# VectorE's one-column reads of kept numbers take a zero from a PSUM bank as their other operand, stand at every step of the left direction too, and are left out of the first 64 steps

## The chip, the cores and the metric

The kernel runs on one core of one Trainium2 chip. The metric is the device time of one execution in microseconds; lower is better. The median of the runs is what is compared.

## The reference, cut to what matters

Four residual layers work on `x` of shape (4, 48, 256, 256), each behind a group norm of 16 groups. Layer 0 is channel attention with a depthwise convolution, layer 1 a gated convolution. Layers 2 and 3 are the ones that the change touches. Both are four scans, one after the other, in which each row or column is the input plus a convolution of five taps along the row or column made just before:

```python
def step(w, b):
    def f(carry, inp):
        nxt = inp + _conv1d(carry, w, b)      # 48 channels to 48, 5 taps
        return (nxt, nxt)
    return f
_, d_rest = scan(step(down_w, down_b), xs[0], xs[1:])         # down, row by row
_, u_rest = scan(step(down_w, down_b), u0, seq)               # up
_, r_rest = scan(step(right_w, right_b), r0, ws[1:])          # right, column by column
_, l_rest = scan(step(left_w, left_b), l0, R[Ww - 2::-1])     # left
x = x + _L2_conv_ref(_gn(x), ...)                             # and the same for layer 3
```

No step of a scan can start before the step ahead of it is done. Each of the four directions has 255 steps, in each of the two layers.

## The kernel before, in words

`layers01` computes the first two layers; its last third overlaps with the beginning of `scans`. `scans` holds layers 2 and 3 (called layer 0 and 1 inside it) as two **chains**: `chain(0)` carries images 0 and 1, `chain(1)` images 2 and 3. Each chain is a generator; `next` on it emits one step. Chain 0 is emitted `lead = 992` steps ahead of chain 1, then both alternate, and chain 1 does its last steps alone, beside `to_rows(0, ...)`, which reorders chain 0's finished output with copies on GpSimd and ScalarE (`oo<-oi`). A planner reorders the emitted instructions on each engine by priority and dependence; the order on each engine is then fixed.

One **step** (`step`) works on the two images of a pair one after the other. For each image, called its first and second half here, TensorE runs three matmuls of 96x128 (in float32 each shows as two records) into a bank of PSUM, and VectorE adds the input to the result and writes it to a `carry` tile (`carry<-ps,dn`, `carry<-ps,up` at L1068; `carry<-ps,pre`, `carry<-ps,lines` at L1072). The matmuls of the next step read that `carry`. There are `NC = 4` carry tiles for a chain, used in turn, so a carry may be overwritten only when everybody has read it. What else reads it depends on the direction:

- down and up: ScalarE writes carry plus bias over the input row (`dn<-carry`, `up<-carry`);
- right: GpSimd first copies the column out of the block into a small tile `pre` (L1259), VectorE adds it, ScalarE writes the line (`lines<-carry`, L1286). Chain 0 has three `pre` tiles, chain 1 four;
- left: GpSimd adds the carry into the block `stage` in place (L1334, 96x256 for both images). In the second layer of chain 1 (`direct`), it adds into `done` instead, one 96x128 add for each image (L1338), and `out<-done` is stored from there. In the first layer, VectorE also takes statistics of the finished block of 16 columns (`st<-stage`, eight instructions for a block).

Around these steps stand **looks**: VectorE instructions on one column whose result, `seen`, nobody uses. A look reads a number that ScalarE or GpSimd has written, so VectorE waits for that engine once there, and the planner then need not give the same wait to VectorE instructions behind it. `look(place, fetched)` keeps the last places in a list and reads the oldest when more than three are kept: a copy (L1039) in down and up, and in right one add (L1041) of the old line and of the `pre` tile that the next step needs. In left, not in `direct`, every second step has a copy of its own (L1348).

```python
kept.append(place)
if len(kept) > 3:
    if fetched is None:
        nc.vector.tensor_copy(seen, kept.pop(0))
    else:
        nc.vector.tensor_add(seen, kept.pop(0), fetched)
```

Of the kernel before, what the change touches and what calls it, by code (L numbers as in the profile page):

```python
# [9 lines left out]
F32 = mybir.dt.float32  # L10
# [3 lines left out]
PSUM = bass.MemoryType.PSUM  # L14
DRAM = bass.MemoryType.DRAM

B, C, H, W = 4, 48, 256, 256
G = 16
NP = 2
P = 96  # L20
# [944 lines left out]
def scans(ctx, tc, xs, out, wts, biases, dram, k, coefs, lead, spare):  # L965
# [13 lines left out]
    nc = tc.nc  # L979
# [3 lines left out]
    pool = lambda name, bufs, **how: ctx.enter_context(  # L983
        tc.tile_pool(name=name, bufs=bufs, reuse_waits="tile", **how)
    )
# [6 lines left out]
    slots_d = pool("c_slot_d", 5)  # L992
    p_small = pool("c_ps", 1, space=PSUM)
    psum = pool("c_psum", 2, space=PSUM)
    sums = [spare, psum]
    buffers = [Ring([slots_a] * 3 + [slots_c, slots_b]), Ring([slots_d] * 5)]
    NT = H // RT
    NH = RT // 2
    CB = 2 * KC
# [16 lines left out]
    def take(pair, name):  # L1016
        return buffers[pair].tile([P, SLOT], F32, tag="slot", name=name)

    def chain(pair):
# [7 lines left out]
        seen = wp.tile([P, 1], F32, tag=f"seen{pair}", name="seen")  # L1027
        kept = []

        def look(place, fetched=None):  # L1030

            kept.append(place)
            if len(kept) > 3:
                if fetched is None:
                    nc.vector.tensor_copy(seen, kept.pop(0))  # L1039
                else:  # L1040
                    nc.vector.tensor_add(seen, kept.pop(0), fetched)  # L1041

        def slot(name):
            return take(pair, f"{name}{pair}")

        def inner():
            return carry[at[0]][:, :, 1 : HP - 1]
# [5 lines left out]
        def blocks(v):  # L1053
            return v.rearrange("p b (k w) -> p b k w", w=KC)
# [30 lines left out]
        def row(ts, r):  # L1085
            return rows_view(ts[r % 2])[:, :, :, r // 2, :]

        def load_rows(layer, n, r, t, k0, k1):

            v = rows_view(t)  # L1090
            for b in range(2):
                for q in range(2):
                    nc.sync.dma_start(
                        v[q * C : (q + 1) * C, b, k0:k1].rearrange("c k h w -> c k (h w)"),
                        xs[layer][pair][
                            r * C : (r + 1) * C, b, 2 * k0 + q : 2 * k1 - 1 + q : 2, n * NH : (n + 1) * NH, :
                        ].rearrange("c k h w -> c k (h w)"),
                    )

        def layer_of(layer, first):  # L1100
# [18 lines left out]
            def norm(t, b):  # L1119
                v = by_batch(t)[:, b]  # L1120
                g = biased[b]
                nc.scalar.activation(v, v, AF.Identity, bias=g[:, 1:2], scale=g[:, 0:1])
# [11 lines left out]
            for n in range(NT):  # L1134
                ahead_ = None
                for r in range(RT):
                    if r == 0:
                        kept.clear()
                        while len(halves) < min(2 * n + 5, 2 * NT):
                            t = slot("dn")  # L1140
                            load_rows(layer, len(halves) // 2, len(halves) % 2, t, 0, NK)
                            halves.append(t)
                        if n + 1 < NT:
                            ahead_ = halves[2 * n + 2 : 2 * n + 4]
                    if ahead_ and r in (11, 14, 22, 25):
                        norm(ahead_[r // 22], r % 11 // 3)
                    inp = row(now, r)

                    def keep(new, b):
                        nc.scalar.activation(inp[:, b], blocks(new[:, b]), AF.Identity, bias=bias[:, 0:1])  # L1150

                    if n == 0 and r == 0:
                        keep(inner(), slice(0, 2))
                    else:
                        step(layer, 0, inp, keep)
                    look(inp[:, 1, 0, 0:1])
                    yield
                if ahead_:
                    for r in range(2):
                        nc.sync.dma_start(D[n][r], now[r])  # L1160
                    now = ahead_
# [90 lines left out]
            fetched = {}  # L1252
# [59 lines left out]
            direct = layer == 1 and pair == NP - 1  # L1312
            done = None
            writes = []
            for n in reversed(range(NK)):
                ahead_ = None
                if direct and n % 2 == 1:
                    done = [take(0, "done") for _ in range(2)]
                for w in reversed(range(CB)):
                    if w == CB - 1 and n > 0:  # L1320
                        ahead_ = slot("lines"), slot("stage")
                        nc.sync.dma_start(ahead_[0], Rt[n - 1])
                        nc.sync.dma_start(by_batch(ahead_[1]), block_of(x, n - 1))
                    if layer == 0 and n == 0 and w == CB // 2:
                        following = [slot("dn"), slot("dn")]
                        for r in range(2):
                            load_rows(1, 0, r, following[r], 1, NK)
                    line = lines_view(lines)[:, w]
                    to = cols_view(stage)[:, :, w % 2, :, w // 2]

                    def keep(new, b):
                        if not direct:
                            if b.stop == 2:
                                nc.gpsimd.tensor_add(to, to, new)  # L1334
                            return
                        for i in range(b.start, b.stop):
                            place = done[i].rearrange("p (h w) -> p h w", w=2 * CB)[:, :, n % 2 * CB + w]
                            nc.gpsimd.tensor_add(place, to[:, i], new[:, i])  # L1338

                    if n == NK - 1 and w == CB - 1:  # L1340
                        keep(inner(), slice(0, 2))
                    else:
                        step(layer, 2, line, keep)
                    if not direct and w % 2:

                        kept.append(to[:, 1, H // 2 - 1 :])
                        if len(kept) > 1:
                            nc.vector.tensor_copy(seen, kept.pop(0))  # L1348
                    if late:
                        late.pop(0)()  # L1350
                    if writes and w % 8 == 4:
                        writes.pop(0)()
                    yield
                if layer == 0:
                    nc.sync.dma_start(block_of(y, n), by_batch(stage))
                elif not direct:
                    v = stage.rearrange("p (b q t n) -> p b q t n", b=2, q=2, t=NY)
                    for b in range(2):
                        for q in range(2):
                            nc.sync.dma_start(result[:, b, :, 2 * n + q], v[:, b, q])  # L1360
                elif n % 2 == 0:

                    def write(b, r, done=done, w0=n * CB):
                        at_rows = out[(2 * pair + b) * C : (2 * pair + b + 1) * C].rearrange(
                            "c (h r w) -> c h r w", r=2, w=W
                        )
                        nc.sync.dma_start(
                            at_rows[:, :, r, w0 : w0 + 2 * CB],
                            done[b][r * C : (r + 1) * C].rearrange("c (h w) -> c h w", w=2 * CB),
                        )  # L1370

                    writes += [lambda b=b, r=r, f=write: f(b, r) for b in range(2) for r in range(2)]
                if layer == 0:

                    def stat(b, c, n=n, v=by_batch(stage)):
                        nc.vector.bn_stats(stats[b][:, n * 4 + c, :], v[:, b, c * 512 : (c + 1) * 512])

                    late += [lambda b=b, c=c, f=stat: f(b, c) for b in range(2) for c in range(4)]
                    if n == 0:
                        for r in range(2):  # L1380
                            for q in range(2):
                                nc.sync.dma_start(
                                    rows_view(following[r])[q * C : (q + 1) * C, :, 0].rearrange("c b h w -> c b (h w)"),
                                    cols_view(stage)[r * C : (r + 1) * C, :, q, :NH, :].rearrange("c b h w -> c b (h w)"),
                                )
                if ahead_:
                    lines, stage = ahead_
# [211 lines left out]
```

## Time and profile before

| What | Value |
|---|---|
| Median of 3 runs | 9099.63 us (9092.13 to 9106.2) |
| Profiled execution, its own time | 9105.24 us |
| Its span, first to last instruction | 9103.5 us |
| Mean granted TensorE clock | 0.984 |
| TensorE matmuls busy | 8713.5 us, 96% of the span |
| VectorE busy | 3971.3 us, 44% |
| ScalarE busy | 3440.2 us, 38% |
| GpSimd busy | 1948.2 us, 21% |
| Looks: L1039, L1041, L1348 | 1852, 1008 and 381 instructions |

The page gives busy time by engine, then the span in 40 slices, then groups of instructions by line with their count, busy time, mean duration and what ended the idle time ahead of them. PE is TensorE, PEld its weight loads, DVE VectorE, ACT ScalarE, POOL GpSimd, SP the queue that issues transfers. Chain 0 begins at about 3200 us beside the end of the second layer and is the only work from about 3600 to 5000 us but for a few steps of chain 1; both chains run from about 5000 to 7750 us; chain 1 is alone from there to the end.

### The profile page before, as it was taken

How to read it: one execution, taken by the hardware profiler on the slowest of the kernel's cores; microseconds unless marked ns; L12 is line 12 of the kernel's file. 1: busy time of each engine (PE TensorE's matmuls, PEld its weight loads, DVE VectorE, ACT ScalarE, POOL GpSimd, SP SyncE). 2: the span in 40 equal slices, each digit the busy share in tenths (PEclk: the TensorE clock that was granted, in tenths of full speed). 3: DMA queues.
4: the chain of work that ended last, by engine and by line, in shares of the span. 5: the costliest groups of instructions: out<-in, count | busy, mean ns of one | idle time of the engine just before them, and what ended most of it. 6: DMA issues, size and time to landing. Idle time of an engine off the chain costs nothing. (4 is left out here: it accounts for less than half of the span.)

```text
span 9103.5 us, 158554 instructions
## 1 busy us (share of the span) xinstructions
PE 8713.5 (96%) x62920; PEld 7234.4 (79%) x62920; DVE 3971.3 (44%) x14031; ACT 3440.2 (38%) x7023; POOL 1948.2 (21%) x3100
## 2 busy tenths in 40 slices
PE   6999999999999978999999999999999999999998
PEld 4777777433333336999888999999999999999998
DVE  3232010234555555444345544444444555444543
ACT  0011000123343455765400776666554002765610
POOL 0000000001111120002444000001445664001566
PEclk9999999999999988999999999999999999999999
DMA  7664323467878877765466755465556787867789
GB/s 150 132 133 89 71 62 73 94 137 168 180 171 179 180 159 163 161 143 143 119 168 165 168 140 135 116 152 134 161 158 163 215 224 175 204 168 191 210 171 184
DMA packets 1180201, 1390.37 MB, mean 153 GB/s; under 512 B 263184, under 2 KB 1107216, under 8 KB 1118784
## 3 DMA queue, kind: packets, MB, share of 16 engines
q1 hardware_dynamic: 1179360, 1379.90, 64.9%
q8 instruction: 493, 8.08, 0.4%
q14 instruction: 252, 2.06, 0.1%
q0 software_dynamic: 96, 0.33, 0.0%
HBM read 811.21 MB, written 509.61 MB: 145 GB/s over the span
## 5 line engine op out<-in xcount | busy, mean ns | idle before, releaser
L1064 PE MATMUL ps<-carry,w 96*96 96x128 f32 x48960 | 5490.2, 274 | 115.0 <-DVE carry L1072 71.7
L1064 PEld LDWEIGHTS ps<-carry,w 96*96 96x96 f32 x48960 | 5407.4, 163 | 207.4 <-DVE carry L1072 134.7
L1259 POOL COPY pre<-col 96x256 f32<-96x256 f32 x1020 | 656.7, 644 | 2755.5 <-DMA col<-last 1971.7
L1150 ACT ACTIVATE dn<-carry,b 96x128 f32<-96x128 f32 (+1 forms) x2044 | 769.1, 398 | 838.3 <-DVE carry L1068 828.9
L1286 ACT ACTIVATE lines<-carry,b 96x128 f32<-96x128 f32 (+1 forms) x2044 | 780.2, 399 | 690.8 <-DVE carry L1072 650.1
L1068 DVE TENSOR_TENSOR carry<-ps,dn 96x128 f32<-96x128 f32 x2280 | 652.5, 287 | 755.8 <-PE ps L1064 730.5
L1194 ACT ACTIVATE up<-carry,b 96x128 f32<-96x128 f32 x1792 | 719.1, 402 | 459.8 <-DVE carry L1068 456.3
L1068 DVE TENSOR_TENSOR carry<-ps,up 96x128 f32<-96x128 f32 x1792 | 516.0, 288 | 598.9 <-PE ps L1064 594.1
L1334 POOL TENSOR_TENSOR stage<-stage,carry 96x256 f32<-96x256 f32 x768 | 656.2, 856 | 527.4 <-DVE carry L1072 497.5
L1072 DVE TENSOR_TENSOR carry<-ps,lines 96x128 f32<-96x128 f32 x2040 | 547.6, 283 | 424.9 <-PE ps L1064 401.1
L581 PE MATMUL py<-x1n,wy 128*96 128x512 f32 x1536 | 703.6, 607 | 30.4 <-ACT x1n L541 27.9
L1072 DVE TENSOR_TENSOR carry<-ps,pre 96x128 f32<-96x128 f32 x2040 | 550.9, 284 | 271.1 <-PE ps L1064 239.7
L295 PE MATMUL acc<-xs,xt 128*96 128x288 f32 x2048 | 666.7, 407 | 0.0
L294 PE MATMUL acc<-xt 128*96 128x288 f32 x2048 | 666.5, 409 | 0.0
L581 PEld LDWEIGHTS py<-x1n,wy 128*96 128x96 f32 x1536 | 245.2, 166 | 455.2 <-issue 437.0
L279 DVE COPY xt<-pt 128x384 f32<-128x384 f32 x256 | 136.6, 554 | 850.8 <-PE pt L276 650.3
L261 ACT ACTIVATE xn<-raw,coef 96x2048 f32<-96x2048 f32 x64 | 133.6, 2094 | 987.6 <-PE pt L276 819.6
L296 PE MATMUL acc<-xt,xs 128*96 128x192 f32 x2048 | 501.7, 327 | 0.0
L296 PEld LDWEIGHTS acc<-xt,xs 128*96 128x96 f32 x2048 | 332.1, 165 | 154.3 <-issue 1.4
L295 PEld LDWEIGHTS acc<-xs,xt 128*96 128x96 f32 x2048 | 332.0, 164 | 151.2 <-issue 2.2
L604 DVE TENSOR_TENSOR y<-py,t 96x512 f32<-96x512 f32 x256 | 171.4, 678 | 600.8 <-PE py L590 600.8
L1041 DVE TENSOR_TENSOR seen<-lines,pre 96x1 f32<-96x1 f32 x1008 | 166.8, 165 | 479.6 <-POOL pre L1259 437.2
(183 smaller groups left out, 5520.3 us busy)
## 6 DMA issues: line engine op xcount, KB each, us to landing
stage<-x SPq DMA_DIRECT2D x64, 1536.0 KB
dn<-x SPq DMA_DIRECT2D x240, 384.0 KB
R<-lines SPq DMA_DIRECT2D x60, 1536.0 KB
lines<-R SPq DMA_DIRECT2D x60, 1536.0 KB
D<-dn SPq DMA_DIRECT2D x56, 1536.0 KB
up<-D SPq DMA_DIRECT2D x56, 1536.0 KB
U<-up SPq DMA_DIRECT2D x224, 384.0 KB
col<-U SPq DMA_DIRECT2D x56, 1536.0 KB
```

The source lines that it names most:

```text
L294: nc.tensor.matmul(acc[0], lhsT=xt[:, h + 2, :], rhs=xt[:, here, :], start=first, stop=last)
L295: nc.tensor.matmul(acc[1], lhsT=xt[:, h + 2, :], rhs=xs[:, here, :], start=first, stop=last)
L296: nc.tensor.matmul(acc[2], lhsT=xs[:, h + 2, :], rhs=xt[:, past, :], start=first, stop=last)
L581: nc.tensor.matmul(ps, lhsT=held["w"][0][:, dx], rhs=x1n[:, 2 * c : 2 * c + 2, dx : dx + W], start=dx == 0, stop=False)
L1064: nc.tensor.matmul(ps, lhsT=w_sb[layer][:, way, j, :], rhs=old[:, i, j : j + W // 2], start=j == 0, stop=j == 2)
L1068: nc.vector.tensor_add(new[:, i].rearrange("p (k w) -> p k w", w=KC), ps.rearrange("p (k w) -> p k w", w=KC), inp[:, i])
L1072: nc.vector.tensor_add(new[:, i], ps, inp[:, i])
L1150: nc.scalar.activation(inp[:, b], blocks(new[:, b]), AF.Identity, bias=bias[:, 0:1])
L1194: nc.scalar.activation(place[:, b], blocks(new[:, b]), AF.Identity, bias=bias[:, 1:2])
L1259: nc.gpsimd.tensor_copy(t, cols_view(block)[:, :, w % 2, :, w // 2])
L1286: nc.scalar.activation(line[:, b], new[:, b], AF.Identity, bias=bias[:, 2:3])
L1334: nc.gpsimd.tensor_add(to, to, new)
```

## The change

A pool with one bank of PSUM is added, and one column of it is set to zero. A look becomes `tensor_add(seen, zero, number)`, with one number of SBUF and the zero from PSUM. Where a look read two numbers (right), it becomes two looks, one for the old line and one for the `pre` tile; the latter now starts with the first step of the direction. In left, the copy at every second step becomes a look at every step, with the list of more than three kept places, on the first row of the column, and there are looks in `direct` too, which had none. The looks of the first 64 steps of chain 0 (down, first layer) are left out.

```diff
     p_small = pool("c_ps", 1, space=PSUM)
     psum = pool("c_psum", 2, space=PSUM)
+    p_zero = pool("c_zero", 1, space=PSUM)
     sums = [spare, psum]
+    zero = p_zero.tile([P, 1], F32, tag="zero", name="zero")
+    nc.vector.memset(zero, 0.0)
...
             kept.append(place)
-            if len(kept) > 3:
-                if fetched is None:
-                    nc.vector.tensor_copy(seen, kept.pop(0))
-                else:
-                    nc.vector.tensor_add(seen, kept.pop(0), fetched)
+            old = [kept.pop(0)] if len(kept) > 3 else []
+            for number in old + ([] if fetched is None else [fetched]):
+                nc.vector.tensor_add(seen, zero, number)
...
                         step(layer, 0, inp, keep)
-                    look(inp[:, 1, 0, 0:1])
+                    if pair or layer or n > 1:
+
+                        look(inp[:, 1, 0, 0:1])
                     yield
...
                         step(layer, 2, line, keep)
-                    if not direct and w % 2:
-
-                        kept.append(to[:, 1, H // 2 - 1 :])
-                        if len(kept) > 1:
-                            nc.vector.tensor_copy(seen, kept.pop(0))
+                    if direct:
+                        look(done[1].rearrange("p (h w) -> p h w", w=2 * CB)[:, 0, n % 2 * CB + w : n % 2 * CB + w + 1])
+                    else:
+                        look(to[:, 1, 0:1])
                     if late:
                         late.pop(0)()
```

## The prediction

> **What bounds the kernel now.** I read the busy times first, then the groups, then the timeline of each stage, since the scans have stages with different limits.
>
> ```profile
> PE   6999999999999978999999999999999999999998
> ...
> L1064 PE MATMUL ps<-carry,w 96*96 96x128 f32 x48960 | 5490.2, 274 | 115.0 <-DVE carry L1072 71.7
> L1334 POOL TENSOR_TENSOR stage<-stage,carry 96x256 f32<-96x256 f32 x768 | 656.2, 856 | 527.4 <-DVE carry L1072 497.5
> L1041 DVE TENSOR_TENSOR seen<-lines,pre 96x1 f32<-96x1 f32 x1008 | 166.8, 165 | 479.6 <-POOL pre L1259 437.2
> ```
>
> TensorE is the bound nearly everywhere: the scan matmuls fill 5490 us and wait 115 us. A VectorE instruction of 0.15 us costs nothing by its own length. What counts is whether a look holds VectorE so long that TensorE runs out of carries. So I read the left direction with both chains, chain 0 in the second layer and chain 1 in the first, in order of time:
>
> ```profile
> 7201.06 0.15 DVE L1348 COPY seen<-stage 96x1 f32<-96x1 f32 x1 [0.97 <-POOL stage L1334]
> 7201.13 0.47 DVE L1072 TENSOR_TENSOR carry<-ps,lines 96x128 f32<-96x128 f32 x2
> 7201.69 0.85 POOL L1334 TENSOR_TENSOR stage<-stage,carry 96x256 f32<-96x256 f32 x1 [0.66 <-DVE carry L1072]
> 7202.57 0.15 DVE L1348 COPY seen<-stage 96x1 f32<-96x1 f32 x1 [0.97 <-POOL stage L1334]
> 7202.64 0.73 DVE L1072 TENSOR_TENSOR carry<-ps,lines 96x128 f32<-96x128 f32 x3
> ...
> 7205.42 0.85 POOL L1334 TENSOR_TENSOR stage<-stage,carry 96x256 f32<-96x256 f32 x1 [0.46 <-DVE carry L1072]
> 7206.31 0.15 DVE L1348 COPY seen<-stage 96x1 f32<-96x1 f32 x1 [0.97 <-POOL stage L1334]
> ```
>
> A look waits 0.97 us for a GpSimd add that began only when the two carries just ahead of the look were done. Look, two carries, add, look: 7201.06 to 7202.57, **1.51 us**. Behind the waiting look stand the other chain's two carries. The looks come every second step: 7201.06 to 7206.31 is 5.25 us for two joint steps (a step of either chain), 2.625 us each, and 24 matmul records of 0.109 us are just that. The steps without looks let VectorE catch up, so TensorE never waits.
>
> The end of the kernel, `direct` left of chain 1 alone, has no looks:
>
> ```profile
> 8850.94 0.29 DVE L1072 TENSOR_TENSOR carry<-ps,lines 96x128 f32<-96x128 f32 x1 [0.39 <-PE ps L1064]
> 8851.31 0.52 POOL L1338 TENSOR_TENSOR done<-stage,carry 96x128 f32<-96x128 f32 x1 [0.15 <-DVE carry L1072]
> 8851.61 0.29 DVE L1072 TENSOR_TENSOR carry<-ps,lines 96x128 f32<-96x128 f32 x1 [0.38 <-PE ps L1064]
> 8851.98 0.52 POOL L1338 TENSOR_TENSOR done<-stage,carry 96x128 f32<-96x128 f32 x1
> ```
>
> Carries follow at 0.67 us, 1.35 us a step, set by TensorE; GpSimd trails and nobody waits for it. Last, the right direction of chain 1 alone, where the other chain's output is reordered:
>
> ```profile
> 8487.45 1.12 POOL L1448 COPY oo<-oi 96x1024 f32<-96x1024 f32 x1
> 8487.54 1.03 DVE L1041 TENSOR_TENSOR seen<-lines,pre 96x1 f32<-96x1 f32 x1 [0.15 <-POOL pre L1259]
> ```
>
> The look, 0.156 us in the median, takes 1.03 us because a GpSimd copy began 0.09 us before it.
>
> [...] a carry, one input from PSUM, keeps its 0.29 us beside GpSimd's `pre` copies. [...] `gn_m<-pg`, one column from PSUM, has a median of 0.146 us against 0.140 for a `seen` copy. I take 0 for the operand [...].
>
> **The change, part by part.** The order in which the changed program's instructions stand, with the instruction that each look waits for, decides. GpSimd's order is unchanged; TensorE, ScalarE and SP differ only at the start of chain 0, where three more of its steps (and some loads of `dn`) stand ahead of the last piece of the layer before. No store or load moves past the looks elsewhere.
>
> 1. *Left with both chains.* Though the source keeps three places back, in the changed order nearly every look waits for the GpSimd add of the step just made, and now both chains have one at every step: look, two carries of chain 0, look, two carries of chain 1. The loop above then closes: 2 x 1.51 = 3.02 us against TensorE's 2.625, +0.395 us. 207 joint steps have chain 0 and chain 1 both in left. Some 35 of them lie beside the statistics (0.68 us each, eight a block) with fewer tight looks; following their order by the same durations I get 12.3 us for four, 3.07 each, so I price all 207 alike: **+82 us**. TensorE now waits for carries; the add on GpSimd is what is late next.
>
> 2. *`direct` left.* 219 of the new looks wait for the second `done` add of the step just made. From a carry's start: 0.37 to GpSimd's start (8850.94 to 8851.31), two adds back to back 1.00 (the trace has such a pair at 8789.08), 0.03 to the look, 0.07 to the carry: 1.47 against 1.35. +0.12 x 219 = +26. Against it, the transfers of this stage run at 98% to 100% of their engines and GpSimd waits 30 us for `stage`; a slower stage gets part of that back, I take 4. **+22 us** (0 to +45: fully hidden by transfers, or each late `stage` block felt at once, where today carries run ahead).
>
> 3. *Left of chain 0 alone.* Today a look at every second step; the cycle of two steps is 3.25 us (looks at 4600.84 and 4604.09), above TensorE's 2.63. With a look at every step, the extra one delays only a first half: its carry starts at 1.58 after the earlier look, not 1.34, while the second half waits for its own matmuls until 1.99, as before. So the next look is again at 3.25. **0**, 0 to +15.
>
> 4. *Right.* Chain 0 alone has a cycle of 3.10 us for two steps, set by a look on the `pre` just copied; this stays. The second look stands between the two carries, 0.08 us, in a step whose other half waits 0.28 us for TensorE. **0**, 0 to +13. With both chains, one tight look is left in a joint step and the loop is near 2.1 us, under 2.6: **0**. With chain 1 alone, the ready line is read in the gap ahead of `pre`: 0.
>
> 5. *Looks no longer blocked by GpSimd.* 15 looks of L1041 took 0.43 to 1.04 us; the ten after 8370 us left weight loads idle by about 0.66 us each: **-7 us** (-10 to -4).
>
> 6. *Start.* 58 looks fewer in down, where TensorE is busy; more carries wait for ScalarE themselves (0.02 us on VectorE's queue); the zero is set once. The three steps in another place may give or take 4 us at the handover. **0**. Down and up keep their looks between two halves, 0.25 us from hurting.
>
> Sum: 82 + 22 - 7 = +97 us. Against the profiled span, 9103.5 + 97 = 9200.5; its own time, 9105.2, becomes 9202. That execution lies 5.6 us above the median, so the median becomes **9197 us**.
>
> **The rivals.**
>
> *The loop closes, but `direct` is covered by its transfers* (98% busy speaks for it; that the carries pace at TensorE's 0.67 speaks against): 9099.6 + 82 - 7 + 2 = 9177. Chance 0.15.
>
> *PSUM reads are dear.* [...] The `gn_m` row speaks against. Chance 0.13.
>
> *The looks do not bind, and the time is not slower.* If they waited for adds two or more steps old, as the three kept places suggest, VectorE would never stand behind GpSimd in left: the stalls of chain 0 alone go, (3.25 - 2.63) / 2 x 250 = 77 us, with the 7: 9015. It decides from one step of distance: with it, the add has 2.6 us to be done instead of none. The resolved waits speak against. Chance 0.04.
>
> *The bound holds everywhere* (the look pair ends under 2.63 us because queues overlap more than the row at 7201 shows): only the 7 us remain, 9093. Chance 0.04.
>
> **How the numbers follow.** The forecast, 9197, has 0.64 of the chance. About 0.2%, 18 us, is what a measurement of this kernel can tell from no change. Faster comes from the third rival, 0.04; same from the fourth, 0.04; slower is the rest, 0.92. The range covers forecast and first two rivals with half the bounds of parts 2 to 4: 9145 to 9260.
>
> **What would show it.** In left with both chains, looks 1.51 us apart throughout, joint steps of 3.02 us and TensorE idle by about 0.4 in each; in `direct`, steps of 1.47 us; no look over 0.2 us beside `oo` copies; `seen` near 0.15 us; chain 0's cycles still 3.25 and 3.10. Joint steps of 2.63 us with looks at every step would prove me wrong; so would looks well above 0.15 us.

## The result, and the profile after

The changed kernel takes **9186.73 us** (9184.77 to 9187.56), the kernel before 9102.1 in the same comparison: a ratio of **1.0094, 95% interval 1.0077 to 1.0112**. The forecast was 9197. The profiled execution has a span of 9184.2 us against 9103.5, 80.7 longer.

To see where, I read the start of each carry (the answers for the tile `carry`, counted off in the order of its chain) and cut both spans at the same carries:

| Stretch | Before | After | Difference | Forecast |
|---|---|---|---|---|
| start of the span to the first carry | 3248.2 | 3241.1 | -7.1 | 0 |
| to the last 64 steps of chain 0's second right | 3652.6 | 3655.3 | +2.7 | 0 |
| to the end of chain 1's first left (64 steps with chain 0 still in right, then left with both chains) | 748.3 | 824.9 | +76.6 | +82 |
| chain 1 alone, to the end of its right | 1075.7 | 1076.4 | +0.7 | -7 |
| `direct` left and the end | 378.7 | 386.5 | +7.8 | +22 |

From the pages, the weight loads of the scans in the kernel before (count, then busy us, mean ns, idle us before it and what ended most of it),

```profile
L1064 PEld LDWEIGHTS ps<-carry,w 96*96 96x96 f32 x48960 | 5407.4, 163 | 207.4 <-DVE carry L1072 134.7
```

and in the changed kernel the matmuls, the weight loads and the add on GpSimd:

```profile
L1066 PE MATMUL ps<-carry,w 96*96 96x128 f32 x48960 | 5605.9, 275 | 89.6 <-DVE carry L1070 30.9
L1066 PEld LDWEIGHTS ps<-carry,w 96*96 96x96 f32 x48960 | 5415.1, 163 | 289.2 <-DVE carry L1074 142.9
...
L1338 POOL TENSOR_TENSOR stage<-stage,carry 96x256 f32<-96x256 f32 x768 | 655.3, 853 | 611.0 <-DVE carry L1074 574.6
```

The matmuls' line hides the lost time: their busy time has grown by 116 us and their idle time is smaller (89.6 us, 115.0 before). In the trace a matmul's record lasts 0.27 us and the next one begins 0.109 us after it began, so a matmul that begins 0.12 us late leaves no gap. The weight loads, with records of 0.163 us, show it: they are idle for 81.8 us more, in a span that is 80.7 us longer. The add on GpSimd waits 611 us instead of 527. The answer for the tile `seen`, its first rows, says what the looks wait for (us, times):

```profile
its engine sat idle before it (us, times) until:
  POOL stage L1338: 541.1, 593
  POOL pre L1263: 408.8, 515
  POOL done L1342: 134.1, 208
```

Before, `stage` held looks for 306.3 us in 361 waits, `done` for none. The timeline of left with both chains, changed kernel, the lines of GpSimd and VectorE for 3 us, and one of the weight loads:

```profile
7401.26 0.15 DVE L1043 TENSOR_TENSOR seen<-zero,stage 96x1 f32<-96x1 f32 x1 [0.96 <-POOL stage L1338]
7401.34 0.47 DVE L1074 TENSOR_TENSOR carry<-ps,lines 96x128 f32<-96x128 f32 x2
7401.67 1.34 PEld L1066 LDWEIGHTS ps<-carry,w 96*96 96x96 f32 x12 [0.18 <-DVE carry L1074]
7401.89 0.85 POOL L1338 TENSOR_TENSOR stage<-stage,carry 96x256 f32<-96x256 f32 x1 [0.66 <-DVE carry L1074]
7402.77 0.15 DVE L1043 TENSOR_TENSOR seen<-zero,stage 96x1 f32<-96x1 f32 x1 [0.96 <-POOL stage L1338]
7402.85 0.47 DVE L1074 TENSOR_TENSOR carry<-ps,lines 96x128 f32<-96x128 f32 x2
7403.40 0.85 POOL L1338 TENSOR_TENSOR stage<-stage,carry 96x256 f32<-96x256 f32 x1 [0.66 <-DVE carry L1074]
7404.29 0.15 DVE L1043 TENSOR_TENSOR seen<-zero,stage 96x1 f32<-96x1 f32 x1 [0.97 <-POOL stage L1338]
```

Look, two carries, add, look: 7401.26, 7402.77, 7404.29. The loop of 1.51 us that stood at every second pair of carries now stands at every one, so a joint step takes 3.03 us by these lines (3.04 on average: 194.4 us for 64 joint steps, against 169.6, or 2.65 each, before), and TensorE's weight loads wait 0.18 us for the carry. And `direct`, the lines of GpSimd and VectorE:

```profile
8790.24 0.15 DVE L1043 TENSOR_TENSOR seen<-zero,done 96x1 f32<-96x1 f32 x1 [0.74 <-POOL done L1342]
8790.32 0.28 DVE L1074 TENSOR_TENSOR carry<-ps,lines 96x128 f32<-96x128 f32 x1
8790.67 1.01 POOL L1342 TENSOR_TENSOR done<-stage,carry 96x128 f32<-96x128 f32 x2 [0.47 <-DVE carry L1074]
8790.77 0.29 DVE L1074 TENSOR_TENSOR carry<-ps,lines 96x128 f32<-96x128 f32 x1 [0.18 <-PE ps L1066]
8791.71 0.15 DVE L1043 TENSOR_TENSOR seen<-zero,done 96x1 f32<-96x1 f32 x1 [0.65 <-POOL done L1342]
```

From look to look 1.47 us; the first half waits for GpSimd, no longer for TensorE.

### The profile page after: what moved, and what is told of

Same layout as the page of the kernel before. It is cut to its first block, busy times and chain, and to the rows that moved or that the text cites. A ratio compares the mean times of both kernels' runs of the same rounds, so it can differ in the third digit from the quotient of the medians.

```text
span 9184.2 us, 159563 instructions
## 1 busy us (share of the span) xinstructions
PE 8824.9 (96%) x62920; PEld 7238.2 (79%) x62920; DVE 4066.6 (44%) x15625; ACT 3442.7 (37%) x7023; POOL 1939.7 (21%) x3100
## 5 line engine op out<-in xcount | busy, mean ns | idle before, releaser
L1066 PE MATMUL ps<-carry,w 96*96 96x128 f32 x48960 | 5605.9, 275 | 89.6 <-DVE carry L1070 30.9
L1074 DVE TENSOR_TENSOR carry<-ps,pre 96x128 f32<-96x128 f32 x2040 | 577.0, 284 | 259.2 <-PE ps L1066 242.7
L590 PE MATMUL py<-x2n,wy 64*96 64x512 f32 x1536 | 363.0, 601 | 0.0
```

The source lines that it names most:

```text
L1066: nc.tensor.matmul(ps, lhsT=w_sb[layer][:, way, j, :], rhs=old[:, i, j : j + W // 2], start=j == 0, stop=j == 2)
L1074: nc.vector.tensor_add(new[:, i], ps, inp[:, i])
```

## The experiments

Theory: a look costs nothing by itself, it costs where VectorE stands at it for work that GpSimd began too late. Rivals: the operand in PSUM costs, `direct` is covered by its transfers, the other parts matter. The edits are against the changed kernel unless said otherwise. Where a time is given "from the first carry", it is the span less the start of the first carry, which leaves out the scatter of the first two layers.

**Left: every second step again.**

```diff
-                    else:
-                        look(to[:, 1, 0:1])
+                    elif w % 2:
+                        kept.append(to[:, 1, H // 2 - 1 :])
+                        if len(kept) > 1:
+                            nc.vector.tensor_add(seen, zero, kept.pop(0))
```

> The changed kernel with the looks of left (not direct) at every second step again, as adds with the PSUM zero. Theory, that two looks at every joint step close a loop of VectorE and GpSimd: left with both chains falls back from 3.04 to 2.65 us a joint step, 207 steps, so 9187 - 79 = 9108 us; direct keeps its 1.44 us a step. Rival, that the sheer number of VectorE instructions or the PSUM operand costs: 380 of 4834 looks are gone, under 10 us of VectorE time, so 9178 to 9187 us.

Measured: 9103.23 us, ratio 1.0007 (0.9999 to 1.0016); 64 joint steps take 169.6 us again. The looks at every step in left are 83 us, and without them no loss is left that the interval shows.

**No looks in `direct`.**

```diff
-                    if direct:
-                        look(done[1].rearrange("p (h w) -> p h w", w=2 * CB)[:, 0, n % 2 * CB + w : n % 2 * CB + w + 1])
-                    else:
+                    if not direct:
                         look(to[:, 1, 0:1])
```

> The changed kernel without the 253 looks in direct. Theory: from there to the end falls from 386 us to the 379 us of the kernel before, steps 1.36 us each, so 9187 - 8 = 9179 us, and carries run ahead of the adds again at late stage blocks. Rival, that the transfers bound this stage: the last block ends when it did, 9187 us.

Measured: 9178.69 us, ratio 1.0083 (1.0068 to 1.0098); `direct` and the end take 379.4 us, as before (378.7), not 386.5. So these looks are worth 7 to 8 us. The answer for the tile `done` shows why not 22 (GpSimd's idle time, us and times), here without the looks,

```profile
  DVE carry L1074: 38.2, 210
  DMA stage<-x: 37.8, 8
```

and here in the changed kernel, with them:

```profile
  DVE carry L1074: 104.8, 220
```

Without looks the scan overtakes the loads of `stage` and waits 37.8 us for them (30.1 in the kernel before); with looks it is slower and never does. Most of the loop's price is paid out of that wait.

**The looks of left alone, put into the kernel before**, as copies of SBUF, no PSUM:

```diff
-                    if not direct and w % 2:
+                    if not direct:

                         kept.append(to[:, 1, H // 2 - 1 :])
-                        if len(kept) > 1:
+                        if len(kept) > 3:
                             nc.vector.tensor_copy(seen, kept.pop(0))
```

> The kernel before with one edit: its copies of left (SBUF, no PSUM zero) stand at every step, three places kept back. Theory, that the count of looks in left is the cause and the operand is not: 9102 + 79 = 9181 us, looks 1.51 us apart in left with both chains, direct unchanged at 1.36 us a step. Rival, that the PSUM operand matters: 9102 us, with left at 2.65 us a joint step.

Measured: 9184.56 us, ratio 1.0093 (1.0078 to 1.0108). The loss is there without any operand in PSUM.

**Looks tied to the newest matmul result**, to make them old in fact: the zero is replaced by a column of the bank that the last carry read.

```diff
+        newest = [zero]
...
-                nc.vector.tensor_add(seen, zero, number)
+                nc.vector.tensor_add(seen, newest[0], number)
...
                 else:
                     nc.vector.tensor_add(new[:, i], ps, inp[:, i])
+                newest[0] = ps[:, 0:1]
                 after(new, b)
```

> The changed kernel with one operand exchanged: a look adds the first column of the newest matmul result in PSUM instead of the zero, so that it can't stand ahead of its own step and reads what was written three steps back. Theory, that it is the distance that costs and not the look: left with both chains 2.63 us a joint step (-79), direct 1.35 (-8), and chain 0 alone loses the stalls that it had before the change too: left 84 us for 64 steps instead of 106, right 84 instead of 99, together 75 to 150 us, so 9187 - 87 - 75 to 150 = 8950 to 9025 us. Rival, that GpSimd's adds and copies are too slow for a step at any distance, or that the banks are now released later: chain 0 alone keeps its 106 and 99 us and the time is near 9100 us or above.

Measured: 9159.55 us, ratio 1.0063 (1.0047 to 1.008), a miss. Left did what was expected, with as many looks as the changed kernel has (4834): 168.0 us for 64 joint steps, 95.9 for 64 steps of chain 0 alone (106.5). But down and up alone went from 84 to 90, chain 1's right alone from 86 to 102.5. The answer for `seen` in that stage (8373 to 8782 us) says who waits for the looks:

```profile
  POOL pre L1265: 223.8, 233
  PEld ps L1067: 66.0, 249
```

A look on a matmul's bank holds the bank: the next step's work on TensorE, here its weight loads, waits for it (249 times, 66.0 us), and the next column's copy on GpSimd waits for the late look too (233 times, 223.8 us). Which of the two sets the 102.5 us is not separated; two kernels below, whose looks read no such bank, take as long in this stage. GpSimd has no part in a step of down or up, so there the bank is what is left. What the expectation mis-sized is the room that the bank had.

**No looks in left at all.**

```diff
-                    if direct:
-                        look(done[1].rearrange("p (h w) -> p h w", w=2 * CB)[:, 0, n % 2 * CB + w : n % 2 * CB + w + 1])
-                    else:
-                        look(to[:, 1, 0:1])
```

> The changed kernel with no look in left at all, direct left included; everything else as changed. Theory (a look closes the loop GpSimd's add into stage -> look -> next carry in left, in chain 0 alone too): left with both chains runs at TensorE's 2.63 us per joint step instead of 3.04 (about -80), direct left as in the kernel before (-8), and chain 0's left alone falls from 106 us per 64 steps to between 87 and 96 (-40 to -77): 9020 to 9060 us. Rival (the looks only take over a wait that the next carry would make itself; without them the carry waits for GpSimd's add, in two instructions of waits): left with both chains stays near 3.0 us per joint step or chain 0's left alone stays at 106, and the time is 9100 or more.

Measured: **9044.89 us, ratio 0.9943 (0.9928 to 0.9958)**: faster than the kernel before. 64 joint steps 168.0 us, which is TensorE's pace (2.625 us each, 24 matmul records 0.109 us apart); 64 steps of chain 0's left alone 95.6. The carries do their own waiting at no price that shows; in the kernel before, a wait that stands ahead of a carry as an instruction of its own (611 times at L1072) takes 0.021 us in the median.

**Looks in the middle of the next step**, between its two carries, with the sums' first column for the zero, two tiles in turn for the result and, in right, the column two steps ahead:

```diff
-            old = [kept.pop(0)] if len(kept) > 3 else []
-            for number in old + ([] if fetched is None else [fetched]):
-                nc.vector.tensor_add(seen, zero, number)
+            due.clear()
+            due.extend([kept.pop(0)] if len(kept) > 2 else [])
+            due.extend([] if fetched is None else [fetched])
...
                 after(new, b)
+                if i == 0:
+                    for to_see, number in zip(seen, due):
+                        nc.vector.tensor_add(to_see, ps[:, 0:1], number)
+                    due.clear()
```

> The changed kernel with its looks moved: each is made inside the following step, right after image 0's carry, as an add with the first column of image 0's sums in PSUM in place of the zero; a number becomes due when more than two are kept, the look in right asks for the prefetched column two steps ahead, and two tiles take the sums in turn, so that a look never stands ahead of a carry that TensorE waits for and asks for work 2 to 3 steps old. Theory (only tight looks cost, a look that is old costs its 0.15 us beside TensorE): left with both chains 2.63 us per joint step (-80), chain 0's right alone from 99 to about 84 us per 64 steps (-60), chain 0's left alone from 106 to 84 to 92 (-56 to -88), other stages as they are, direct about -8: 8950 to 8990 us. Rival (the look between the two carries of a step delays image 1's carry by 0.15 to 0.3 us wherever one chain runs alone, and holds image 0's bank): down and up alone go from 84 to 89 or more per 64 steps, chain 1's right alone from 87 to 95 or more, and the time is 9060 to 9130.

Measured: 9126.69 us, ratio 1.0033 (1.0019 to 1.0048). Both sides were half right: left with both 168.0, chain 0's right 90.4 and left 97.0; but down and up alone 89.5 and chain 1's right 90. Two neighbouring lines of up, this kernel (3952 us),

```profile
3951.79 0.29 DVE L1071 TENSOR_TENSOR carry<-ps,up 96x128 f32<-96x128 f32 x1 [0.46 <-PE ps L1067]
3952.00 0.14 DVE L1079 TENSOR_TENSOR seen<-ps,up 96x1 f32<-96x1 f32 x1
```

and the changed kernel there:

```profile
3951.19 0.29 DVE L1070 TENSOR_TENSOR carry<-ps,up 96x128 f32<-96x128 f32 x1 [0.36 <-PE ps L1066]
3951.40 0.14 DVE L1043 TENSOR_TENSOR seen<-zero,up 96x1 f32<-96x1 f32 x1
```

The look stands in the same place and is no longer. It reads a row one step younger, already written, and takes its other operand from the matmul's bank; the next carry waits 0.10 us more for its sums (0.46 for 0.36). So the bank explains the 5.5 us in 64 steps, and a bank of its own for the zero avoids them. The kernel with looks tied to the newest result has the same 0.46 us here.

**The looks of the first 64 steps back** (the condition `if pair or layer or n > 1` taken out).

> The changed kernel with the looks of the first 64 steps back (as adds with the zero in PSUM). Theory (leaving these looks out is what brought chain 0 to the end of its first way down 6 to 7 us earlier): it gets there 6 to 7 us later again, 9193 to 9194 us. Rival (the earlier start comes from something else, such as another order of the first loads): chain 0 gets there as in the changed kernel, and the time is 9187.

Measured: 9188.78 us, ratio 1.0099 (1.0084 to 1.0115), and from the first carry 5942.3 against 5943.1 us. The rival holds. The 7 us lie before the first carry: it comes between 3230.9 and 3248.9 us in the profiled executions of the fourteen kernels, and at 3235.2 in this one, which has the looks. TensorE's instructions up to there stand in the same order in all fourteen; two of the kernels, the one before and the one with the looks of left alone, differ in the text of left only and begin at 3248.2 and 3233.4 us.

**The zero in SBUF.**

```diff
-    p_zero = pool("c_zero", 1, space=PSUM)
-    zero = p_zero.tile([P, 1], F32, tag="zero", name="zero")
+    zero = wp.tile([P, 1], F32, tag="zero", name="zero")
```

> The changed kernel with its zero in a tile of SBUF instead of a bank of PSUM; nothing else. Theory (a look with both operands in SBUF is held up by GpSimd's copies of the last stage, one with an operand in PSUM isn't): in the last stage some looks take about 1 us again, as in the kernel before, and the idle time of TensorE there rises from 4 us to 6 to 10: 9188 to 9197 us; everywhere else the looks last about 0.15 us and the stages don't move. Rival (where the zero lies is of no account): no look over 0.2 us and 9187 us.

Measured: 9221.01 us, ratio 1.0137 (1.0122 to 1.0152), from the first carry 33 us more than the changed kernel. The timeline of the last stage, this kernel:

```profile
8567.55 1.12 POOL L1451 COPY oo<-oi 96x1024 f32<-96x1024 f32 x1
8567.73 0.95 DVE L1043 TENSOR_TENSOR seen<-zero,pre 96x1 f32<-96x1 f32 x1
```

The look begins inside the GpSimd copy and ends with it (8568.67 and 8568.68). 552 of its 4834 looks last over 0.2 us; of the changed kernel's, none does. The theory holds and was too small: it named the last stage alone, but looks are held by GpSimd's shorter instructions too: 476 of the 552 end just after a `pre` copy (0.22 us in the median), 23 after a `done` add (0.44) and 18 after a `stage` add (0.29). Against the changed kernel, left with both chains takes 16 us more, the stretches before and after it, and `direct`, 6 each. Not all of it is the hold: the planner also orders VectorE's looks otherwise in places, and 13.5 of the 16 us fall in 64 steps at the beginning of left, where tight looks begin earlier, as in the kernel with the looks of left alone (12.4). How much of the 33 us either has is not separated.

**Right without the look at the line.**

```diff
-                        look(line[:, 1, 0:1], fetched[n * CB + w + 1][:, 1, 0:1])
+                        look(fetched[n * CB + w + 1][:, 1, 0:1])
```

> The changed kernel with one look fewer in a step of right: only the one at GpSimd's next column, none at ScalarE's line. Theory (the second look of right waits for a line whose activation is queued behind ScalarE's copy of the output, and this took back the 7 us that the unblocked looks gave): right of chain 1 alone loses 1 to 2 us of each 64 steps, 6 to 7 us in all, everything else stays: 9180 us. Rival (the column, not the line, is what right of chain 1 waits for once no look is blocked): that stage stays within 1 us and the time is 9186 to 9188.

Measured: **9260.95 us, ratio 1.0185 (1.0169 to 1.02)**, a clear miss of both: chain 1's right alone takes 102 to 103 us for 64 steps where two looks took 86. With the edit the column goes through the list of kept numbers, so in the source it is read three steps late; in the order on VectorE, it isn't. The answers for `seen` in this stage, what the looks waited for, changed kernel (8450 to 8800 us),

```profile
  POOL pre L1263: 8.3, 18
```

and without the line's look (8462 to 8869):

```profile
  POOL pre L1263: 192.9, 239
```

**No looks in left and right** (the `look` of right taken out as well).

> The changed kernel with no look in left and none in right: looks are left in down and up alone. To be read against the kernel with no look in left (9044.9 us). Theory (as in left, a look in chain 0's right asks one step before the carry needs it for GpSimd's next column, and so shortens the loop over GpSimd by about a step; the carry can do its own waiting): chain 0's right alone goes from 99 us per 64 steps to between 86 and 92 (-30 to -52), chain 1's right alone keeps its 84 to 88: 8993 to 9015 us. Rival (in right the carry needs the look, since it would have to wait for GpSimd's column and TensorE's sums in two instructions): chain 0's right gains nothing and chain 1's goes to 90 or more: 9045 to 9070.

Measured: **9008.84 us, ratio 0.9909 (0.9893 to 0.9926)**, the best version. Chain 0's right alone takes 88.5 us for 64 steps instead of 99.4, chain 1's 88.5 instead of 86; the gain outweighs the loss four to one.

**No looks anywhere.**

> The changed kernel with no look anywhere. To be read against the one with looks in down and up alone. Theory (a look is worth nothing in this kernel: down and up alone are full of TensorE at 84.2 us per 64 steps with them and stay so without): no difference over 5 us between the two. Rival (in down and up the look does move a wait for ScalarE off the carry, whose own waits then take two instructions between the last matmul and the next): down and up alone go to 87 to 90 us per 64 steps, about 13 such stretches, +35 to +75 us against the other.

Measured: 9016.34 us, ratio 0.9913 (0.9898 to 0.9928): by the medians not to be told from the kernel above. The stages do tell a little: down takes 1 to 3 us more for 64 steps, up 84.0 as ever. Looks in down may be worth some 10 us (from the first carry 5774.2 against 5764.5), well under the 35 to 75 us of the rival.

**A column's look at once, in chain 1's right alone**, on top of the kernel with looks in down and up:

```diff
                         step(layer, 1, fetched.pop(n * CB + w), keep)
+                    if pair and (n + 1 < NK or w + 1 < CB):
+                        nc.vector.tensor_add(seen, zero, fetched[n * CB + w + 1][:, 1, 0:1])
```

> The kernel with looks in down and up alone (9008.8 us), with one look more: in chain 1's right, at the end of each step, at GpSimd's next column as soon as it is asked for (not three steps late, as in the kernel without the look at the line); none at ScalarE's line. Theory (the look at the line, behind ScalarE's copies of the output, is what kept chain 1's right from gaining when the looks stopped being blocked): chain 1's right alone runs at TensorE's 84 us per 64 steps, 336 to 339 us for its four stretches against 353.9 with no look and 343.9 with both looks: 8993 to 8998 us. Rival (the column itself comes late, or the carry waits for the line then): the four stretches take 343 us or more, and the time is 8998 to 9010.

Measured: 9071.4 us, ratio 0.9972 (0.9961 to 0.9984). The stage takes 407 us in its four stretches, as in the kernel without the line's look, so how late the source reads the column is of no account. Its timeline:

```profile
8401.25 0.29 DVE L1074 TENSOR_TENSOR carry<-ps,pre 96x128 f32<-96x128 f32 x1 [0.19 <-PE ps L1066]
8401.67 0.64 POOL L1263 COPY pre<-col 96x256 f32<-96x256 f32 x1 [1.01 <-DVE carry L1074]
8402.35 0.15 DVE L1301 TENSOR_TENSOR seen<-zero,pre 96x1 f32<-96x1 f32 x1 [0.81 <-POOL pre L1263]
8402.43 0.64 DVE L1074 TENSOR_TENSOR carry<-ps,pre 96x128 f32<-96x128 f32 x2
```

The order of the instructions explains it. In both kernels the look stands right behind the carry of image 1 that frees the column's tile, and waits for the copy that waits for this carry: carry, copy, look, carry, with nothing between. The column is the one that the scan needs four steps later; the look has no need to be there. In the changed kernel the same look stands behind the *next* step's first carry, after the look at the line, and finds the column ready. Both write the one tile `seen`, so their order is fixed between them. That this is what held the column's look back is argued from the order; a kernel with two separate tiles and two free looks was not tried.

## Why the prediction was right, and where its sizes were off

The mechanism and the sign hold, and the total is 10 us off (9186.73 for 9197; as a difference to the kernel before, 84.6 us for 97.4). Part of this closeness is luck: term 2 was 14 us too high and term 4 was 8 us too low, so they cancel in part. The terms:

1. *Left with both chains*, +82: measured 76.6 in the cut, 83 by putting it back. The loop of 2 x 1.51 us closed as worked out, at 194.4 us for 64 joint steps (3.04 each). The same loss without PSUM, none without looks, and none with as many looks that ask for older work (168.0 us) show that the tight look is the cause. TensorE's pace of 2.625 us was not quite reached before, at 2.65 a joint step.
2. *`direct`*, +22: measured +8. The step of 1.47 us was nearly right for the first 128 steps (93.6 and 92.1 us for 64, or 1.46 and 1.44 a step, against 86.8 twice); at that pace 219 looks cost about 21 us, not 26. The term that was mis-sized most is the 4 us given back by transfers: of the 21, some 13 did not arrive (both are estimates from these stretches). The rows had shown it, as GpSimd waited 30.1 us for `stage` in that stage. The rival that had it wholly covered said 2.
3. *Left of chain 0 alone*, 0: +0.3 us for 64 steps. *Right of chain 0 alone*, 0: -0.1.
4. *Looks no longer blocked*, -7: the looks did become short (none over 0.157 us; with the zero in SBUF, looks of up to 1.03 us are back in this stage), but the stage gained nothing (345.0 against 344.4 us). The price of a hold was right: before, nine times in this stage a matmul began 0.61 to 0.67 us late behind a look of 1.02 to 1.04 us, 5.7 us in all, and none of these is left. What the term left out is the wait behind it: the look asks for a `pre` copy, and this copy stands on GpSimd behind `oo` copies, whether VectorE is held or not. One such place in the changed kernel (only the lines of this chain of waits):

```profile
8636.85 1.12 POOL L1451 COPY oo<-oi 96x1024 f32<-96x1024 f32 x1
8637.90 0.64 POOL L1263 COPY pre<-col 96x256 f32<-96x256 f32 x1
8638.58 0.15 DVE L1043 TENSOR_TENSOR seen<-zero,pre 96x1 f32<-96x1 f32 x1 [1.22 <-POOL pre L1263]
8638.99 6.07 PEld L1066 LDWEIGHTS ps<-carry,w 96*96 96x96 f32 x40 [0.95 <-DVE carry L1074]
```

   Four times a matmul begins 0.42 to 1.14 us late so, 3.1 us in all; before, such a wait without a hold came once, 0.44 us. Just behind the place shown, from 8639.5 to 8642.7 us, the granted clock is 0.50 and 15 matmuls begin 0.213 us apart instead of 0.109: 1.6 us more. This slow stretch stands at the same step in all five kernels with two looks in a step of right and the zero in PSUM, and in none of the others; no run shows why. About 1 us more is in the first steps of `direct`, which the cut counts here. My first reason for the missing gain, the line's look behind ScalarE's copies, fell: without that look the stage is 63 us longer (407.8).
5. *Start*, 0: right (-0.8 us by putting the looks back, from the first carry). The -7.1 us ahead of the first carry lie within the scatter of the layers before. They took the span of this execution further from the forecast: from the first carry on it is 87.8 us longer, for the +97 of the sum.

That a look with one operand outside SBUF is not held, on which term 4 rested, no look of the kernel before had shown; the carries beside GpSimd's `pre` copies, at 0.29 us, were the nearest to it. The kernels with the zero in PSUM and in SBUF show it: in the first a look that begins 0.11 us into an `oo` copy of 1.14 us takes 0.15 us (at 8560.22 us) and none is over 0.157 us, in the second the look of 0.95 us at 8567.73 us ends with the copy that it began in. The rival with dear PSUM reads, whose price no trace had shown, is not seen: looks with the zero in PSUM last 0.144 to 0.155 us in the median, with it in SBUF 0.145 to 0.155 in the median as well.

The rival that put looks two steps back, 9015 us, had the right idea of where time lay: the kernel without looks in left and right takes 9009. It failed as a forecast because the source's age of a number is not its age in the order.

Open: what holds right without looks at 88.5 us for 64 steps and left of chain 0 alone at 95.6, above TensorE's 84. In right, the trace names ScalarE's line ahead of every other carry (104.9 us in 225 waits from 4180 to 4500 us); no kernel changed that.

## What to carry to other kernels

An instruction that only takes over waits is as dear as the youngest work that it asks for, and a planner that puts each instruction where its operand first exists makes it ask for the youngest: read in the final order what each such look waits for, and what that in turn waits for, whatever the source keeps back. If the loop so closed (here 2 x 1.51 us) is longer than the bound engine's step (2.625), it becomes the bound; try the kernel without looks first. A freed wait is worth only what the next wait at the same place leaves of it, so follow the chain one link further (here to the column's copy behind GpSimd's other copies), and look for a transfer that is waiting behind the stage. Where matmul records overlap (here 0.27 us long and 0.109 us apart), measure TensorE's lost time by the spacing of the matmuls or by the idle time of the weight loads: the idle time of the matmuls fell by 25 us while the kernel lost 81.

## What was not expected of the hardware

- In the kernel with the zero in SBUF, a VectorE add of one column with both operands there is held up by GpSimd's short instructions too, not by its long copies alone: it lasts 0.22 us in the median where it ends with a `pre` copy (0.64 us) and 0.29 with a `stage` add (0.85 us), against 0.145 to 0.155 in the medians of all looks by tile.
- Reading one column of a matmul's bank after the carry has read it delays the next sums into that bank by 0.10 us (the carry waits 0.46 us for them instead of 0.36), enough for 5.5 us in 64 steps where TensorE is the bound.
- Profiled executions differ by up to 18 us in the start of the first carry, with TensorE's instructions in the same order up to there: a difference of a few us between two spans has to be cut there before it is explained.
